# A four-layer convolution network on one core: layer 2's pass issued in the order of its text, with other lags and a split norm chain

## The chip, the core and the metric

The kernel runs on one core of one Trainium2 chip. The metric is the device time of one execution, in microseconds (us). Five engines of the core matter here: TensorE (PE) for matrix products and transposes, VectorE (DVE), ScalarE (ACT), GpSimd (POOL), and SyncE (SP), which issues every DMA of this kernel. Each engine has its own queue of instructions, and an instruction that needs another engine's result waits on a semaphore.

## The reference, cut to what matters

`x` has 16 images of 64 x 64 tokens with 256 channels. Four layers follow one another, each of the form `x = x + layer(group_norm(x))`:

```python
x = x + L0(_gn(x))   # linear attention with a layer norm
x = x + L1(_gn(x))   # gates per channel and per token, batch norm over all images, relu
x = x + L2(_gn(x))   # involution, 3 x 3, kernels made per token
x = x + L3(_gn(x))   # involution, 7 x 7, kernels made per token

def _gn(v, G=32, eps=1e-5):
    g = v.reshape(B_, H_, W_, G, C_ // G)
    m = jnp.mean(g, axis=(1, 2, 4), keepdims=True)
    s = jnp.var(g, axis=(1, 2, 4), keepdims=True)
    return ((g - m) / jnp.sqrt(s + eps)).reshape(v.shape)

# L2, K = 3, 16 groups of kernels
r = relu(bn(x @ Wr + br)); w = (r @ Ws + bs).reshape(B, H, W, 16, 1, 9)
# patches: nine shifted copies of (x @ Wi + bi), reshaped to (B, H, W, 16, 16, 9)
out = jnp.sum(w * patches, axis=-1)
```

Layer 1's batch norm needs sums over all images before its output can be made, and each group norm needs the sums of a whole image. So the kernel goes over the images in several passes.

## The kernel before, in words

The kernel has four stages. The first does layer 0 and gathers layer 1's maps, the second does layer 1's scan and its batch statistics, the third is layer 2's pass, and the last is layer 3. The change lies in the third stage, whose loop begins at line 1144.

The third stage cuts an image into 8 pieces of 512 tokens, so there are 128 pieces. One turn `n` of the loop works on four pieces at once, each of another age. `LAG = (0, 9, 17, 27)` says how old: `jobs(n)` (line 1127) gives the piece whose layer 1 is ended in this turn (`end`), the piece that is projected by `Wi` (`proj`, 9 turns later), the piece whose involution is computed (`inv`, 17 turns later), and the piece that is centred and stored in strips for layer 3 (`cen`, 27 turns later). The parts of a turn are these:

- `end_of_layer1` (line 891) is a generator with three parts. Part one is two DVE instructions (L899) that make `z`. Part two is two ACT relus (L905) and two POOL additions (L908) that make `x2`. Part three is two statistics of `x2` on DVE (L914), which wait for POOL. In the text before, part three of a turn stands near the start of the next turn.
- `projected` (L948 on PE, L952 on ACT) fills the lines of `pad`.
- `prepare` makes the next piece ready: `reduced2` (L969 on PE, L972 on ACT), 36 transposes of `pad` on PE in nine tiles `pt` (L995), copied by ACT to `xs` (L999, with short copies at L1001 and L1005), and `weights` (L979). It stands early in the turn, except where the next piece is the first of an image; there it stands after the products.
- `residual` (L1021, L1023) puts the piece's `x2` into the two accumulators `lo`. `products` multiplies patches and weights on DVE (24 instructions L1033 in a turn, 12 for each half). `sums` adds nine taps on DVE (L1045) and adds the result to `lo` (L1046). For a quarter of the first half, PE adds the taps (`sums_on_tensor`, L1050), and ACT copies that quarter to `x3` at the next turn (L1175).
- `turned` transposes the `x3` of the turn before (L1060 on PE, L1061 on ACT), and `statistics3` takes its statistics on DVE (L1080).
- `centred` subtracts the channel means `gmb` on POOL (L1103) and leaves 32 small DMAs to be issued by SP.

Twice in an image a norm chain runs: `norm2`, when the last piece of an image has ended layer 1, and `norm3`, when the last piece has its `x3`. Both begin with `group_norm` (line 109): DVE gathers statistics (L114), PE averages over groups (L117), DVE takes deviations (L119 to L123), PE averages again (L126), and DVE and POOL take the inverse root (L98, L99). `norm2` then scales the weights on DVE (L924, L925) and has a PE product `pm` (L931) and two DVE instructions (L936, L938). `norm3` ends with a PE product `pb` (L1095) and a DVE copy of it to `gmb` (L1098), a tile with a single buffer. The chains are generators too; each call of `step()` in the loop runs one more link of every chain that is open. A turn has six such calls, called S1 to S6 below, in the order of the text.

What sets the order on an engine: the framework's scheduler. It takes the text as a priority and orders each engine's instructions by its own model of time, so the order in the queues is not that of the text. It also hands out buffers.

The PSUM pools of this stage are `tr` with 2 buffers, `sm` with 1 (for the norm chains' small products and for `reduced2`), `pw` with 3 and `acc` with 2.

Of the kernel before, what the change touches and what calls it, by code (L numbers as in the profile page):

```python
# [9 lines left out]
F32 = mybir.dt.float32  # L10
# [3 lines left out]
PSUM = bass.MemoryType.PSUM  # L14

P = 128
C = 256
# [3 lines left out]
CT = 512  # L21
# [23 lines left out]
def network(ctx: ExitStack, tc: tile.TileContext, a: dict, out: bass.AP):  # L45
    nc = tc.nc
# [61 lines left out]

    def group_norm(stats, pool):


        mv = small.tile([P, 2, 2], F32, tag="gn_mv", name="gn_mv")
        for h in range(2):
            nc.vector.bn_aggr(mv[:, h, :], stats[:, h].rearrange("p n s -> p (n s)"))  # L114
        yield
        pg = pool.tile([P, CT], F32, tag="sm", name="pg")
        nc.tensor.matmul(pg[:, 0:2], lhsT=gmat, rhs=mv[:, :, 0], start=True, stop=True)  # L117
        gm = small.tile([P, 2], F32, tag="gn_m", name="gn_m")
        nc.vector.tensor_copy(gm, pg[:, 0:2])  # L119
# [29 lines left out]
    with ExitStack() as st:  # L149
# [304 lines left out]
        def gate1(i):  # L454

            mv, gm, rstd = yield from group_norm(st1.pop(i), sm)
            av = small.tile([P, 2, 2], F32, tag="av", name="av")
# [364 lines left out]
    with ExitStack() as st:  # L822
# [95 lines left out]
        def norm2(i):  # L918

            _, gm, rstd = yield from group_norm(st0.pop(i), sm)  # L920
            wrs = wk.tile([P, 2, 64], F32, tag="wrs", name="wrs")
# [4 lines left out]
            yield  # L926
            pm = sm.tile([P, CT], F32, tag="sm", name="pm")
            for f in range(3):
                for h in range(2):
                    lhsT = wrs[:, h] if f == 2 else w[:, h, f * P : (f + 1) * P]  # L930
                    nc.tensor.matmul(  # L931
                        pm[0 : 64 if f == 2 else P, f : f + 1], lhsT=lhsT, rhs=gm[:, h : h + 1],
                        start=(h == 0), stop=(h == 1),
                    )
            b2 = small.tile([64, 1], F32, tag="b2", name="b2")
            nc.vector.tensor_scalar(b2, pm[0:64, 2:3], sb2[0:64, 2:3], sb2[0:64, 1:2], ALU.mult, ALU.add)  # L936
# [25 lines left out]
        def reduced2(i, rc):  # L962
# [160 lines left out]

        LAG = (0, 9, 17, 27)
        TURNS = NI * NCH + LAG[3]

# [14 lines left out]

        loads(0)
        ahead, made, ending, last_end = None, None, None, None
        for n in range(TURNS):
            end, proj, inv, cen = jobs(n)
            nxt = jobs(n + 1)[2]
            done, stores[:] = list(stores), []
            loads(n + 1)
            for dst, src in done:
                nc.sync.dma_start(out=dst, in_=src)  # L1150
            nxt_cen = jobs(n + 1)[3]
            if nxt_cen:
                load_centred(*nxt_cen)
            now, ahead = ahead, None
            last_end, ending = ending, end_of_layer1(*end) if end else None
            if ending:
                next(ending)
            if last_end:
                next(last_end, None)
            if inv:  # L1160
                w1 = weights(now[1], 1)
                x3 = wk.tile([P, 4, C], F32, tag="x3", name="x3", bufs=3)
            step()

            def prepare():
                x2r, rt = reduced2(*nxt)
                ahead = [x2r, rt]
                ahead.append(patches(*nxt, lambda: ahead.append(weights(rt, 0))))
                return ahead

            if nxt and nxt[1]:
                ahead = prepare()
            step()
            if made:
                nc.scalar.copy(made[2][:, 0:ON_PE, 0:P], made[3][:, 0:ON_PE])  # L1175
            if ending:
                next(ending)
            if inv:
                los = residual(now[0])
            c3 = turned(*made[:3]) if made else None  # L1180
            step()
            if proj:
                projected(*proj)
            if inv:
                pd = products(0, now[2], now[3])
                sums_on_tensor(pd, los[0])
            step()
            if nxt and not nxt[1]:
                ahead = prepare()
            if inv:  # L1190
                pd1 = products(1, w1, now[3])
                sums(0, pd, los[0], x3)
            if made:
                statistics3(*made[:2], c3)
            step()
            if inv:
                sums(1, pd1, los[1], x3)
            made = (*inv, x3, los[0]) if inv else None
            step()
            if cen:  # L1200
                centred(*cen)
        for dst, src in stores:
            nc.sync.dma_start(out=dst, in_=src)

# [308 lines left out]
```

## Time and profile before

| quantity | us |
|---|---|
| median of 3 runs | 11259.85 |
| lowest and highest run | 11252.87, 11263.24 |
| the profiled execution's own time | 11230.29 |
| its span, first to last instruction | 11228.4 |
| first instruction L899 of layer 2's pass | 4169.2 |
| last instruction L1103 of layer 2's pass | 8019.5 |

Layer 2's pass takes some 3850 us of the 11228. The profiled execution is 29.6 us below the median of the runs; both of its numbers differ from each other by 1.9 us that lie around the span.

The views used below are these. The page's second part cuts the span into 40 slices of 281 us; layer 2's pass lies in slices 15 to 28, counted from zero. The table by windows gives the busy time of each engine in a stretch. The timeline lists instructions in order of time: start, duration, engine, line, operation, what is written and read, and in brackets the idle time before it with what ended it. The list of waits sums such idle times.

### The profile page before, as it was taken

The numbers are of one execution on the slowest core, as the hardware profiler recorded it, in microseconds if no ns is written. First come the engines' busy times: TensorE is split into PE (matmuls) and PEld (weight loads), VectorE is DVE, ScalarE is ACT, GpSimd is POOL, SyncE is SP. The second block draws the span as 40 slices with busy tenths as digits, with TensorE's granted clock in tenths as the row PEclk, the third lists the DMA queues.
The fourth block names the chain that finished last, engine by engine and source line by source line (L and its number), as shares of the span: only waits on it lengthen the run. The fifth ranks groups of instructions, "written<-read, shape, count | busy, mean of one in ns | idle before, by whom it ended". The sixth has DMA issues, their size and how long they took to land.

```text
span 11228.4 us, 218020 instructions
## 1 busy us (share of the span) xinstructions
PE 8510.5 (76%) x88184; PEld 6175.2 (55%) x88184; DVE 7531.5 (67%) x11694; ACT 4699.1 (42%) x10571; POOL 1065.1 (9%) x681
## 2 busy tenths in 40 slices
PE   8889888988886407777777777777277777778777
PEld 5666666666664205555555555555165656666555
DVE  5566656656665498988888888899254545555444
ACT  4555555555554004333333333333144444444444
POOL 0110111111110001111111111111000000000000
PEclk9999999999997558888888888888689998998988
DMA  7334334434432385555555555544356555555555
GB/s 239 129 134 148 130 122 146 139 128 133 145 101 84 106 279 177 160 169 165 163 159 167 160 168 164 163 151 141 107 177 202 185 194 179 179 181 176 195 185 171
DMA packets 1353714, 1796.58 MB, mean 160 GB/s; under 512 B 132875, under 2 KB 1031812, under 8 KB 1351556
## 3 DMA queue, kind: packets, MB, share of 16 engines
q1 hardware_dynamic: 1352708, 1782.63, 49.6%
q8 instruction: 697, 11.42, 0.4%
q14 instruction: 309, 2.53, 0.1%
HBM read 1268.05 MB, written 536.87 MB: 161 GB/s over the span
## 4 chain that ended last, share of the span: by engine, by line
PE 32%; DVE 20%; issue 17%; DMA 10%; ACT 9%; SPq 7%; POOL 4%; POOLq 0%; DVEq 0%; ACTq 0%
PE pa L1347 6%; DVE wm L1303 6%; SPq L1150 5%; PE pq L261 5%; PE pk L1288 4%; PE py L417 4%; DMA c_d<-c 3%; DVE x L1045 3%; PE pr L1256 2%; ACT sq L426 2%; ACT wm L1298 2%; DVE pd L1033 2%; PE px L948 2%; PE pt L995 2%; DMA xc<-x_d 1%
## 5 line engine op out<-in xcount | busy, mean ns | idle before, releaser
L261 PE MATMUL pq<-wq,xn 128*128 128x384 f32 x4096 | 1475.9, 500 | 59.8 <-DVE diag L310 20.9
L1033 DVE TENSOR_TENSOR pd<-xs,pw 128x576 f32<-128x576 f32 (+15 forms) x3072 | 1450.5, 544 | 47.7 <-ACT xs L1001 47.7
L1303 DVE TENSOR_TENSOR wm<-pk,spanb 128x704 f32<-128x704 f32 x896 | 1148.4, 1344 | 217.4 <-PE pk L1288 217.1
L1288 PE MATMUL pk<-rt,span 64*128 64x176 f32 x12288 | 1175.6, 329 | 153.5 <-DVE wm L1303 61.0
L1347 PE MATMUL pa<-wm,xw 126*32 126x48 f32 x45056 | 819.6, 227 | 474.2 <-issue 374.1
L1288 PEld LDWEIGHTS pk<-rt,span 64*128 64x128 f32 x12288 | 938.1, 188 | 385.7 <-ACT wm L1298 181.8
L1298 ACT ACTIVATE wm<-pk,spanb 128x176 f32<-128x176 f32 x2560 | 975.0, 542 | 337.8 <-PE pk L1288 328.9
L1045 DVE TENSOR_REDUCE x<-pd 128x384 f32<-128x3456 f32 (+1 forms) x256 | 1109.2, 4334 | 0.0
L1347 PEld LDWEIGHTS pa<-wm,xw 126*32 126x32 f32 x45056 | 679.8, 124 | 714.2 <-issue 516.7
L1357 DVE SCALAR_TENSOR_TENSOR ex<-pa,msk,ex 128x192 f32<-128x192 f32 x704 | 287.2, 416 | 1161.8 <-ACT ex L1356 1159.3
L261 PEld LDWEIGHTS pq<-wq,xn 128*128 128x128 f32 x4096 | 752.8, 194 | 492.5 <-issue 54.1
L995 PE MATMUL pt<-ident,pad 128*128 128x128 f32 x4608 | 759.7, 310 | 244.2 <-ACT pad L952 188.5
L995 PEld LDWEIGHTS pt<-ident,pad 128*128 128x128 f32 x4608 | 593.4, 160 | 422.0 <-ACT pad L952 234.2
L1050 PE MATMUL lo<-pd,ident 128*128 128x128 f32 x2304 | 568.0, 415 | 285.4 <-DVE pd L1033 285.4
L999 ACT COPY xs<-pt 128x512 f32<-128x512 f32 x1152 | 644.8, 586 | 299.1 <-PE pt L995 264.4
L1356 ACT ACTIVATE ex<-pa,msk 128x192 f32<-128x192 f32 x704 | 289.3, 420 | 1019.2 <-PE pa L1347 1016.1
L1050 PEld LDWEIGHTS lo<-pd,ident 128*128 128x128 f32 x2304 | 501.2, 268 | 335.6 <-DVE pd L1033 315.3
L948 PE MATMUL px<-x2p,wis 128*128 128x512 f32 x1024 | 571.7, 708 | 37.5 <-ACT c L1061 23.2
L972 ACT ACTIVATE rt<-pr,b,sb 64x512 f32<-64x512 f32 x128 | 98.9, 772 | 1077.3 <-PE pr L969 1017.5
L417 PE MATMUL py<-wo,oT 128*128 128x256 f32 x2048 | 482.4, 386 | 59.9 <-DVE va L277 45.2
L417 PEld LDWEIGHTS py<-wo,oT 128*128 128x128 f32 x2048 | 378.8, 191 | 135.3 <-PE po L380 49.0
L426 ACT ACTIVATE sq<-y 128x256 f32<-128x256 f32 x512 | 213.2, 416 | 520.2 <-DVE y L422 511.7
(229 smaller groups left out, 13427.4 us busy)
## 6 DMA issues: line engine op xcount, KB each, us to landing
xw<-strips SPq DMA_DIRECT2D x704, 512.0 KB
xn<-x_d SPq DMA_DIRECT2D x256, 512.0 KB
x<-x_d SPq DMA_DIRECT2D x256, 512.0 KB
x_d<-x SPq DMA_DIRECT2D x256, 512.0 KB
strips<-xc SPq DMA_DIRECT2D x3072, 28.0 KB
xin<-in_x SPq DMA_DIRECT2D x256, 256.0 KB
x_d<-xc SPq DMA_DIRECT2D x128, 512.0 KB
xm<-x_d SPq DMA_DIRECT2D x128, 512.0 KB
```

Of the source, the lines that this page charges most:

```text
L261: nc.tensor.matmul(pq[:, dd, 0:384], lhsT=xn[:, h, tok], rhs=wq[:, h, hf * 384 : (hf + 1) * 384], start=(h == 0), stop=(h == 1),)
L417: nc.tensor.matmul(py[:, q, :], lhsT=oT[hf][:, q * P : (q + 1) * P], rhs=wo[:, hf, :], start=(hf == 0), stop=(hf == 1),)
L948: nc.tensor.matmul(px, lhsT=w[:, h, fh * P : (fh + 1) * P], rhs=x2[:, h], start=(h == 0), stop=(h == 1),)
L995: nc.tensor.transpose(pt[:, k, h * P : (h + 1) * P], lines[:, h, rc * 4 + e + k, 2 * j : 2 * j + P], ident,)
L999: nc.scalar.copy(t[:, e : e + 2, 0:C], pt)
L1033: nc.vector.tensor_tensor(pd[:, :, o - oh * P : o - oh * P + n, :], xs[dj][:, di : di + 4, c0 : c0 + 9 * n].rearrange("p r (f k) -> p r f ...
L1045: nc.vector.tensor_reduce(half, pd[:, n:], AX.X, ALU.add)
L1050: nc.tensor.matmul(lo[:, 0:ON_PE], lhsT=ident, rhs=pd[:, 0:ON_PE, :, k], start=False, stop=(k == 8))
L1288: nc.tensor.matmul(pkv[:, b, m], lhsT=span[half, h * 8 + q * 2 + gg, s0 : s0 + P], rhs=rto[half, o, :], start=True, stop=True,)
L1298: nc.scalar.activation(dst[:, m // 2, m % 2], pkv[:, m // 2, m % 2], AF.Identity, bias=spanb[:, g0 + m : g0 + m + 1],)
L1303: nc.vector.tensor_tensor(dst, pkv, spanb[:, g0 : g0 + 4].rearrange("p (b m) -> p b m", b=2).unsqueeze(3).broadcast_to([P, 2, 2, NTL]), AL ...
L1347: nc.tensor.matmul(pav[32 * q : 32 * q + 32, :, tj * TC : (tj + 1) * TC], lhsT=xws[k][0:TILE_IN, tj, 32 * q : 32 * q + 32], rhs=wm[q][0:TI ...
```

## The change

Three things change in layer 2's pass.

1. The whole loop stands in `tc.manual_schedule()`. Inside it every engine, SP with its DMAs included, issues its instructions in the order of the text. Buffers are still handed out by the scheduler.
2. The norm chains of this pass are split: `apart=True` puts a link on PE and the DVE link that reads its result at different calls of `step()`, and one call without work follows the inverse root. The lags become `(0, 10, 18, 29)`, so there are 157 turns where there were 155. The pool `sm` goes, and its tiles come from `tr`, which has 3 buffers now.
3. Part three of `end_of_layer1` moves from the start of the next turn to the end of its own turn, after `sums(1, ...)`. Part two now stands ahead of the ACT copy L1175, which stood ahead of it.

The diff, without the lines of the loop that are only indented and without the calls in layers 0 and 1, which pass `"sm"` as the tag:

```diff
-    def group_norm(stats, pool):
+    def group_norm(stats, pool, tag, apart=False):
         mv = small.tile([P, 2, 2], F32, tag="gn_mv", name="gn_mv")
         for h in range(2):
             nc.vector.bn_aggr(mv[:, h, :], stats[:, h].rearrange("p n s -> p (n s)"))
         yield
-        pg = pool.tile([P, CT], F32, tag="sm", name="pg")
+        pg = pool.tile([P, CT], F32, tag=tag, name="pg")
         nc.tensor.matmul(pg[:, 0:2], lhsT=gmat, rhs=mv[:, :, 0], start=True, stop=True)
+        if apart:
+            yield
         gm = small.tile([P, 2], F32, tag="gn_m", name="gn_m")
...
         yield
-        pv = pool.tile([P, CT], F32, tag="sm", name="pv")
+        pv = pool.tile([P, CT], F32, tag=tag, name="pv")
         nc.tensor.matmul(pv[:, 0:2], lhsT=gmat, rhs=dev, start=True, stop=True)
+        if apart:
+            yield
         rstd = small.tile([P, 2], F32, tag="gn_r", name="gn_r")
         inv_sqrt(rstd, pv[:, 0:2], GN_EPS)
         yield
+        if apart:
+            yield
         return mv, gm, rstd
...
-        tr = st.enter_context(tc.tile_pool(name="b_tr", bufs=2, space=PSUM))
-        sm = st.enter_context(tc.tile_pool(name="b_sm", bufs=1, space=PSUM))
+        tr = st.enter_context(tc.tile_pool(name="b_tr", bufs=3, space=PSUM))
...
-            _, gm, rstd = yield from group_norm(st0.pop(i), sm)
+            _, gm, rstd = yield from group_norm(st0.pop(i), tr, "tr", apart=True)
...
-            pm = sm.tile([P, CT], F32, tag="sm", name="pm")
+            pm = tr.tile([P, CT], F32, tag="tr", name="pm")
...
+            yield
             b2 = small.tile([64, 1], F32, tag="b2", name="b2")
...
-            pr = sm.tile([P, CT], F32, tag="sm", name="pr")
+            pr = tr.tile([P, CT], F32, tag="tr", name="pr")
...
-            _, gm, rstd = yield from group_norm(st3.pop(i), sm)
+            _, gm, rstd = yield from group_norm(st3.pop(i), tr, "tr", apart=True)
...
-            pb = sm.tile([P, CT], F32, tag="sm", name="pb")
+            pb = tr.tile([P, CT], F32, tag="tr", name="pb")
...
+            yield
             nc.vector.tensor_copy(gmb[i], pb[:, 0:C])
...
-        LAG = (0, 9, 17, 27)
+        LAG = (0, 10, 18, 29)
...
+        with tc.manual_schedule():
...
-                last_end, ending = ending, end_of_layer1(*end) if end else None
+                ending = end_of_layer1(*end) if end else None
                 if ending:
                     next(ending)
-                if last_end:
-                    next(last_end, None)
...
-                if made:
-                    nc.scalar.copy(made[2][:, 0:ON_PE, 0:P], made[3][:, 0:ON_PE])
                 if ending:
                     next(ending)
+                if made:
+                    nc.scalar.copy(made[2][:, 0:ON_PE, 0:P], made[3][:, 0:ON_PE])
                 if inv:
                     los = residual(now[0])
...
                 if inv:
                     sums(1, pd1, los[1], x3)
+                if ending:
+                    next(ending, None)
                 made = (*inv, x3, los[0]) if inv else None
                 step()
```

A turn of the text after the change runs so: the loads of the next turn, the stores of the turn before and the load for the next `centred`; part one of `end_of_layer1`; `weights` for the second half; S1; `prepare`, if the next piece isn't the first of an image; S2; part two of `end_of_layer1`; the copy L1175; `residual`; `turned`; S3; `projected`; `products` of half 0; `sums_on_tensor`; S4; `prepare`, if the next piece is the first of an image; `products` of half 1; `sums` of half 0; `statistics3`; S5; `sums` of half 1; part three of `end_of_layer1`; S6; `centred`.

More of the change, by code (lines that the diff above doesn't have):

```diff
@@ L232, in norm0 @@
         def norm0(i):
-            _, gm, rstd = yield from group_norm(st0.pop(i), sm)
+            _, gm, rstd = yield from group_norm(st0.pop(i), sm, "sm")
             nb = small.tile([P, 2], F32, tag="gn_b", name="gn_b")
@@ L454, in gate1 @@
         def gate1(i):
-            mv, gm, rstd = yield from group_norm(st1.pop(i), sm)
+            mv, gm, rstd = yield from group_norm(st1.pop(i), sm, "sm")
             av = small.tile([P, 2, 2], F32, tag="av", name="av")
@@ L918, in norm2 @@
         def norm2(i):
-            _, gm, rstd = yield from group_norm(st0.pop(i), sm)
+            _, gm, rstd = yield from group_norm(st0.pop(i), tr, "tr", apart=True)
             wrs = wk.tile([P, 2, 64], F32, tag="wrs", name="wrs")
@@ L1140, in loads @@
                 load_layer1(*end)
[L1142 to L1149, printed above, removed]
-                nc.sync.dma_start(out=dst, in_=src)
[L1151 to L1154, printed above, removed]
-            last_end, ending = ending, end_of_layer1(*end) if end else None
-            if ending:
-                next(ending)
-            if last_end:
-                next(last_end, None)
[L1160 to L1173, printed above, removed]
-            if made:
-                nc.scalar.copy(made[2][:, 0:ON_PE, 0:P], made[3][:, 0:ON_PE])
[L1176 to L1201, printed above, removed]
@@ L1202, in network, with prepare @@
-        for dst, src in stores:
-            nc.sync.dma_start(out=dst, in_=src)
+        with tc.manual_schedule():
+            loads(0)
+            ahead, made = None, None
+            for n in range(TURNS):
+                end, proj, inv, cen = jobs(n)
+                nxt = jobs(n + 1)[2]
+                done, stores[:] = list(stores), []
+                loads(n + 1)
+                for dst, src in done:
+                    nc.sync.dma_start(out=dst, in_=src)
+                nxt_cen = jobs(n + 1)[3]
+                if nxt_cen:
+                    load_centred(*nxt_cen)
+                now, ahead = ahead, None
+                ending = end_of_layer1(*end) if end else None
+                if ending:
+                    next(ending)
+                if inv:
+                    w1 = weights(now[1], 1)
+                    x3 = wk.tile([P, 4, C], F32, tag="x3", name="x3", bufs=3)
+                step()
+                def prepare():
+                    x2r, rt = reduced2(*nxt)
+                    ahead = [x2r, rt]
+                    ahead.append(patches(*nxt, lambda: ahead.append(weights(rt, 0))))
+                    return ahead
+                if nxt and nxt[1]:
+                    ahead = prepare()
+                step()
+                if ending:
+                    next(ending)
+                if made:
+                    nc.scalar.copy(made[2][:, 0:ON_PE, 0:P], made[3][:, 0:ON_PE])
+                if inv:
+                    los = residual(now[0])
+                c3 = turned(*made[:3]) if made else None
+                step()
+                if proj:
+                    projected(*proj)
+                if inv:
+                    pd = products(0, now[2], now[3])
+                    sums_on_tensor(pd, los[0])
+                step()
+                if nxt and not nxt[1]:
+                    ahead = prepare()
+                if inv:
+                    pd1 = products(1, w1, now[3])
+                    sums(0, pd, los[0], x3)
+                if made:
+                    statistics3(*made[:2], c3)
+                step()
+                if inv:
+                    sums(1, pd1, los[1], x3)
+                if ending:
+                    next(ending, None)
+                made = (*inv, x3, los[0]) if inv else None
+                step()
+                if cen:
+                    centred(*cen)
+            for dst, src in stores:
+                nc.sync.dma_start(out=dst, in_=src)
```

## The prediction

> **What bounds the kernel now.** I read the page's slices first, then a table by windows, then the timeline of single turns. The change touches layer 2's pass alone (slices 15 to 28); there DVE is the busiest engine:
>
> ```profile
> DVE  5566656656665498988888888899254545555444
> ```
>
> Windows of that pass: an early turn, a later turn, twice eight turns (one image), and a turn at the end, when layer 1 has run out. The columns are the window, its length, then busy time (and count) of PE, PEld, DVE, ACT, POOL, clock, DMA share, GB/s.
>
> ```profile
> 4335.04:4359.64 24.60, 21.06 (x98) 15.48 (x99) 23.92 (x35) 10.09 (x20) 2.51 (x2) 0.86 0.43 146
> 5301.53:5328.98 27.45, 20.33 (x99) 14.88 (x99) 24.70 (x35) 10.20 (x21) 4.81 (x3) 0.88 0.57 174
> 5424.11:5658.94 234.83, 171.76 (x814) 123.03 (x814) 204.65 (x298) 81.29 (x163) 39.89 (x26) 0.84 0.53 161
> 5658.94:5895.20 236.26, 170.30 (x814) 120.65 (x814) 204.60 (x299) 82.19 (x163) 39.93 (x26) 0.85 0.55 166
> 7623.69:7645.60 21.91, 18.80 (x101) 13.07 (x100) 21.91 (x31) 8.51 (x18) 2.36 (x1) 1.00 0.54 161
> ```
>
> So an image takes 235.5 us, of which DVE works 204.6 and idles some 30. Where it idles, DVE's timeline of the later turn tells:
>
> ```profile
> 5306.38 0.75 DVE L1033 TENSOR_TENSOR pd<-xs,pw 128x576 f32<-128x576 f32 x1
> 5307.05 0.68 DVE L1046 TENSOR_TENSOR x<-x,lo 128x512 f32<-128x512 f32 x1
> 5307.64 10.56 DVE L1033 TENSOR_TENSOR pd<-xs,pw 128x468 f32<-128x468 f32 x23
> 5318.13 0.74 DVE L899 SCALAR_TENSOR_TENSOR z<-x,gm,pf 128x512 f32<-128x512 f32 x1
> 5318.90 0.75 DVE L899 SCALAR_TENSOR_TENSOR pf<-x,gm,pf 128x512 f32<-128x512 f32 x1
> 5321.84 0.69 DVE L914 BATCH_NORM_STATS2 st<-x 128x6 f32<-128x512 f32 x1 [2.18 <-POOL x L908]
> 5323.06 0.69 DVE L914 BATCH_NORM_STATS2 st<-x 128x6 f32<-128x512 f32 x1 [0.53 <-POOL x L908]
> 5323.68 3.74 DVE L1045 TENSOR_REDUCE x<-pd 128x384 f32<-128x3456 f32 x1
> ```
>
> The scheduler puts the statistics L914 right behind their own `z`, and DVE waits 2.7 us for ACT and POOL. The list of waits for an image names the same:
>
> ```profile
> DVE st L914 <- POOL x L908: 22.1, 15, 4.1
> DVE b L936 <- PE pm L931: 3.2, 1, 3.2
> DVE pd L1033 <- ACT xs L1001: 2.7, 2, 1.7
> ```
>
> PE's blocks in that pass, for the queue walk below (matmul records are twice the matmuls in f32):
>
> ```profile
> 5312.69 4.39 PE L1050 MATMUL lo<-pd,ident 128*128 128x128 f32 x18 [2.15 <-DVE pd L1033]
> 5317.01 1.93 PE L969 MATMUL pr<-x2r,wrs 128*64 128x512 f32 x4
> 5319.81 2.00 PE L979 MATMUL pw<-ws,rt 65*128 65x72 f32 x16 [0.87 <-ACT rt L972]
> 5321.68 3.70 PE L948 MATMUL px<-x2p,wis 128*128 128x512 f32 x8
> ```
>
> [...] So in text order one waiting matmul holds all of PE's later work; the [2.15 <-DVE pd L1033] above shows PE so held. [...] with waits before it the block L948 took up to 6.63 us (at 5382.63) against 3.70. [...] here the POOL additions take 1.26 to 1.28 us beside DVE's products too (4347.39), so I count nothing for it.
>
> **The change part by part.** *Steady turn, statistics moved.* The early turn is 24.5 us of DVE without the wait. Text order costs a little: L1046 follows its own reduce directly. Starts 5389.90 and 5394.88 lie 4.98 apart where the second depends on the first, 4.86 (5358.28, 5363.14) where another stands between; 0.12 for each of two pairs. So a turn is 24.7 us if nobody keeps DVE waiting, against 27.45. The additions for L914 are then done some 15 us before DVE comes to them.
>
> *Does the text keep PE in time?* From DVE's start T of a turn: z to 1.3, half 0 of L1033 to 6.9, half 1 to 12.5, reduce to 16.3. There L1046 needs PE's L1050 (an early turn shows it waiting for PE, 0.27 us at 4333.96). PE in text order: ACT's relus end at 2.2, L1175 at 2.5, `residual` 1.4 (eight transposes like L1060's 1.2) to 4.0, `turned` 1.2 to 5.2, L948 to 8.9, L1050 to 13.3; three us to spare. Then `weights` 1.0, L969 1.9, nine tiles paced by ACT (nine copies of 0.55, three short ones of 0.23, the relu of rt 0.77, PE's second `weights` 1.0 between): 9.1 from L969 to ACT's end. PE's and ACT's whole loop is 23.2, only 1.5 below DVE's 24.7. SP: a turn without layer 1 is 21.0 us of issuing (7604.7 to 7625.7), five DMAs of 0.5 more and the wait for the last strips make about 25, below the mean turn found next.
>
> *The chains* are where text order bites. With m = n mod 8:
> - m=0: PE's pg stands at S1, ahead of `prepare`; its statistics come at the very end of DVE's turn m=7. PE stands idle some 10 us, starts `prepare` at T+0.5 instead of T-10, and everything behind it is late: ACT's relus 11.0 (behind the copies), `residual`, `turned`, pv at 14.4. DVE wants pv at S4, behind half 0, at 7.7: stall 6.8. [...] Links' own work: 1.9 (four at 0.2, one 0.2, L924/L925 0.9). Turn 34.9.
> - m=1: pm waits for L925 at the turn's end; DVE 0.7 more. 25.4.
> - m=2: the late `prepare` of m=1 and the early one of m=2 follow each other on PE; L1050 ends at 19.1, wanted at 16.3: stall 2.9, L114 0.6. 28.2.
> - m=3: pg holds PE until L114; pv comes behind `prepare`, at 3.8, wanted at 2.1: stall 1.8[...], links 1.7. 28.7.
> - m=4: the copy L1098 to `gmb` stands at S1, but `gmb` has one buffer, and POOL reads the old one in `centred` of piece 7 of the image before, which falls into this same turn (28+8i with lag 29), at its end. Before, the copy came a good 20 us after that read (5449.83+2.35, then 5472.42), free of charge. Now DVE waits behind ACT's copies (4.1), relus, two additions of 1.27 and `centred` 2.35: to 9.9, from 1.3: 8.6[...]. 34.7.
> - m=5, 6: 24.7 each. m=7: 25.4.
>
> Sum 226.7 against 235.5: 8.8 less an image. Eleven images lie so (turns from 4718 to 7308): -97. In the first sixteen turns before had hardly a wait (199.1 and 208.6 us for eight, L1045 to L1045); with the same stalls but no `centred` I get +22. The last 23 turns, where L914 is gone: about +5. Two turns more: one at the start, 7 us (z to z is 5 to 7), one of strips alone at the end, 15.2 (five from 7907.8 to 7983.9). Sum: -97 + 22 + 5 + 22 = -48.
>
> Against the profiled execution's own 11230.3 that is 11182; it lies 29.6 below the median of the runs, and since the pass has the same shape I move the median alike: 11260 - 48 = **11212**.
>
> **Costs not seen before.** The wait for `gmb`: 5.2 if PE isn't late, 8.6 as walked, nothing if the wait isn't there; I take 8.6, since one buffer excludes nothing. The stall on pv: 0 if PE reaches S3 by 7.7, 10 if `prepare` is slow; 6.8. A third `tr` buffer: gains at most 0.1 a tile (pairs of tiles come 1.33 apart, the copies alone 1.07), or loses 3 us an image if a pt gets the slot that pg holds; I take 9.1 for `prepare`. The links moved apart cost SP nothing; SP's loads stand behind the wait for `x2p`'s buffer (projected at T+9 to 19), one turn before they are needed.
>
> **The rivals.**
> - Gapless: the split chains hide every wait. For: that is 204.6 busy of 234.8 already. Against: pg ahead of `prepare`. An image is 8 x 24.7 + 5.5 = 203, 32 less; eleven give -354, the rest about -12: 10894.
> - `gmb` doesn't wait, the rest as forecast: -11 x 9.6: 11212 - 106 = 11106.
> - Slower: the PE and ACT loop paces every turn. In an early turn ACT took 9.7 us from the relu of rt to the last short copy (4334.81 to 4344.55), where I count 7.2; such a loop is 25.7. Then PE never catches up after a link, and L1046 waits in every turn. With 26 the image is 8 x 26 + 25 (pg 8, pm 9, pg and pb 5, gmb 3) = 233: -27 over eleven, +40 early, +12 late, +22: +47, 11307. It decides from a loop of about 25.5.
> - The whole is no change: the -48 needs only 4 us more an image.
>
> **How the numbers follow.** Forecast 0.50 (its own range 11120 to 11270), `gmb` free 0.10, gapless 0.15, slower 0.25. The range takes in the forecast, the free `gmb` and the slow loop, 11060 to 11330, and leaves out gapless. A measurement of this kernel tells no change from about 0.2%, 22 us: faster 0.63 (most of the forecast, gapless, `gmb` free), same 0.12, slower 0.25.
>
> **What would show it.** L914 without a wait for POOL, and turns of 24.7 between chains: the moved statistics. L98 waiting for pv some 7 us once an image, L1046 waiting for L1050 at m=2, and L1098 waiting for POOL L1103 some 8 us: the text's price. If the sum of DVE's idle time is under 8 us an image, gapless is right; if L1046 waits for PE in every turn, the slow loop is. The forecast is wrong if PE reaches pv early, or SP's queue starves z.

## The result, and the profile after

The kernel after the change takes 11302.34 us (median of 7 runs, 11286.83 to 11311.8) where the kernel before takes 11259.85. The ratio is 1.0037, with a 95% interval of 1.0025 to 1.0049: the change makes the kernel slower by 0.37%, 42.5 us. The forecast was 48 us faster.

The profiled execution of after took 11310.92 us (span 11309.1), 80.7 more by its span than the one of before. Of these, 35 lie in layer 2's pass and 46 in layer 3, whose code is the same: there single profiled executions differ (3139 to 3185 us from its first `wm` to the end, over all kernels of this study). The medians differ by 42.5, so the 35 of the pass would be most of it. The pass, cut at the starts of the 128 long reduces (128x512, L1045 before, L1051 after):

| stretch of the pass | before, us | after, us | difference | forecast |
|---|---|---|---|---|
| span's start to first long reduce | 4310.4 | 4311.6 | +1.2 | +7 |
| first two images | 407.8 | 429.0 | +21.3 | +22 |
| eleven full images | 2590.2 | 2549.4 | -40.8 | -97 |
| the rest, to the last long reduce | 567.9 | 578.6 | +10.7 | +5 |
| last long reduce to layer 3's first `wm` | 212.9 | 255.3 | +42.5 | +15.2 |
| sum | | | +35.0 | -48 |

So the first two images came out as forecast, the start and the end of the images each missed by some 6 us, the full images won less than half of what they should, and the tail (the last row but one) lost almost three times its price. That the tail's 42.5 equals the difference of the medians is chance.

What the move of the statistics was meant to remove is gone. DVE's timeline in a turn without a chain, after (columns as before: start, duration, engine, line, operation, what is written and read):

```profile
5509.02 1.28 DVE L919 BATCH_NORM_STATS2 st<-x 128x6 f32<-128x512 f32 x2
5510.22 0.73 DVE L904 SCALAR_TENSOR_TENSOR z<-x,gm,pf 128x512 f32<-128x512 f32 x1
5510.99 0.75 DVE L904 SCALAR_TENSOR_TENSOR pf<-x,gm,pf 128x512 f32<-128x512 f32 x1
5511.65 8.44 DVE L1039 TENSOR_TENSOR pd<-xs,pw 128x576 f32<-128x576 f32 x18
```

No bracket stands at L919, and none at the other instructions of that turn: DVE works without a pause, and the turn is 24.9 us (forecast 24.7) instead of 27.45. Run e7 below asks whether it was the move that did this. The table by windows for one image, and the list of DVE's waits in the same stretch:

```profile
5433.20:5665.30 232.10, 171.15 (x814) 128.54 (x814) 202.10 (x299) 81.71 (x162) 40.02 (x26) 0.82 0.54 166
```

```profile
DVE isq L98 <- PE pv L128: 16.5, 2, 9.0
DVE gmb L1105 <- POOL xc L1110: 11.3, 1, 11.3
DVE b L942 <- PE pm L936: 0.7, 1, 0.7
```

DVE idles 232.1 - 202.1 = 30 us of an image, as much as before. The 22.1 us of waiting for POOL's additions are gone, and 28.5 us of waiting in the two chains have come. The timeline shows the first wait of `norm3`. PE first:

```profile
5433.39 0.56 PE L117 MATMUL pg<-gn_mv,gmat 128*128 128x2 f32 x2 [4.43 <-DVE gn_mv L114]
...
5435.70 3.27 PE L975 MATMUL pr<-x2r,wrs 128*64 128x512 f32 x4
...
5441.54 1.73 PE L1001 MATMUL pt<-ident,pad 128*128 128x128 f32 x8 [1.99 <-DVE gn_m L121]
...
5449.25 0.28 PE L128 MATMUL pv<-gn_d,gmat 128*128 128x2 f32 x2
```

DVE in the same stretch, with the wait for the means' buffer a turn later:

```profile
5441.34 0.15 DVE L121 COPY gn_m<-pg 128x2 f32<-128x2 f32 x1
...
5449.57 0.16 DVE L98 TENSOR_SCALAR isq<-pv 128x2 f32<-128x2 f32 x1 [7.50 <-PE pv L128]
...
5486.45 0.42 DVE L1105 COPY gmb<-pb 128x256 f32<-128x256 f32 x1 [11.25 <-POOL xc L1110]
```

PE stands 4.43 us before `pg`, whose input DVE makes late in its turn. All of `prepare` follows `pg` in the text, and it now starts late and runs slowly (`pr` 3.27 us, where 1.93 was read before). A transpose `pt` then waits 1.99 us more for the buffer that `pg` holds until DVE reads it at L121. Only behind all this comes `pv`, and DVE has waited 7.50 us for it.

In the tail SP's queue stands still (engine SPq, the issue of DMAs; x32 is a count):

```profile
7801.63 15.35 SPq L1158 DMA_DIRECT2D strips<-xc  x32
7841.38 0.40 SPq L1225 DMA_DIRECT2D wr<-in_w_reduce  x1
7841.82 0.47 SPq L1225 DMA_DIRECT2D span<-in_span  x1
7842.52 1.51 SPq L872 DMA_DIRECT2D xc<-x_d  x2
```

L1225 loads constants of layer 3, code that stands below the loop. The scheduler, which still orders what lies outside the loop, put such loads among the loop's own transfers, here the first two of them. The first waits 24 us, from 7816.98 to 7841.38 (SP's list of waits names PE's product `pw`, L985, of the loop), and the loads and stores of the last turns wait behind it.

### The profile page after: what moved, and what is told of

Read it like the earlier page. It is cut to its first block, busy times and chain, and to the rows that moved or that the text cites. A ratio compares the mean times of both kernels' runs of the same rounds, so it can differ in the third digit from the quotient of the medians.

```text
span 11309.1 us, 218547 instructions
## 1 busy us (share of the span) xinstructions
PE 8498.6 (75%) x88184; PEld 6264.6 (55%) x88184; DVE 7501.0 (66%) x11694; ACT 4692.4 (41%) x10571; POOL 1064.8 (9%) x681
## 4 chain that ended last, share of the span: by engine, by line
PE 35%; DVE 21%; issue 13%; DMA 11%; ACT 9%; SPq 7%; POOL 3%; DVEq 0%; ACTq 0%; POOLq 0%
PE pa L1355 6%; DVE wm L1311 6%; SPq L1158 6%; PE pq L267 5%; PE pk L1296 4%; PE py L423 4%; DVE pd L1039 3%; DMA c_d<-c 3%; PE px L954 2%; DVE x L1051 2%; DMA x_d<-x 2%; PE pr L1264 2%; ACT sq L432 2%; ACT wm L1306 2%; SPq L872 2%
## 5 line engine op out<-in xcount | busy, mean ns | idle before, releaser
L1051 DVE TENSOR_REDUCE x<-pd 128x384 f32<-128x3456 f32 (+1 forms) x256 | 1110.0, 4336 | 0.0
L1005 ACT COPY xs<-pt 128x512 f32<-128x512 f32 x1152 | 608.9, 587 | 149.1 <-PE pt L1001 146.7
L1001 PE MATMUL pt<-ident,pad 128*128 128x128 f32 x4608 | 633.2, 293 | 34.1 <-DVE gn_m L121 22.7
L1001 PEld LDWEIGHTS pt<-ident,pad 128*128 128x128 f32 x4608 | 541.9, 151 | 209.0 <-issue 131.0
L1056 PE MATMUL lo<-pd,ident 128*128 128x128 f32 x2304 | 554.2, 410 | 56.5 <-DVE pd L1039 56.5
L1056 PEld LDWEIGHTS lo<-pd,ident 128*128 128x128 f32 x2304 | 480.9, 218 | 160.3 <-DVE pd L1039 69.2
L954 PE MATMUL px<-x2p,wis 128*128 128x512 f32 x1024 | 529.5, 664 | 8.8 <-ACT pf L910 5.0
L1029 PE MATMUL lo<-ident,x2r 128*128 128x128 f32 x896 | 204.4, 361 | 398.5 <-ACT x L1183 247.9
L117 PE MATMUL pg<-gn_mv,gmat 128*128 128x2 f32 x128 | 29.5, 300 | 620.9 <-DVE gn_mv L114 615.9
```

The source lines that it names most:

```text
L954: nc.tensor.matmul(px, lhsT=w[:, h, fh * P : (fh + 1) * P], rhs=x2[:, h], start=(h == 0), stop=(h == 1),)
L1001: nc.tensor.transpose(pt[:, k, h * P : (h + 1) * P], lines[:, h, rc * 4 + e + k, 2 * j : 2 * j + P], ident,)
L1051: nc.vector.tensor_reduce(half, pd[:, n:], AX.X, ALU.add)
L1056: nc.tensor.matmul(lo[:, 0:ON_PE], lhsT=ident, rhs=pd[:, 0:ON_PE, :, k], start=False, stop=(k == 8))
```

## The experiments

All ratios are to runs of the kernel before on the same chip; "image" is the time of eight long reduces in the middle of the pass, in the profiled execution.

| run | what it is | median, us | ratio [95%] | image, us |
|---|---|---|---|---|
| before | | 11259.85 | 1 | 235.5 |
| after | the change | 11302.34 | 1.0037 [1.0025, 1.0049] | 232.1 |
| e5_statlate | before, statistics moved, scheduler's order | 11261.43 | 0.9998 [0.9989, 1.0007] | 235.5 |
| e7_textonly | before, text order | 11238.45 | 0.9980 [0.9973, 0.9988] | 227.0 |
| e4_nomanual | after, scheduler's order | 11342.58 | 1.0088 [1.0073, 1.0103] | 242.3 |
| e1_sp | after, SP's order kept | 11271.34 | 1.0024 [1.0014, 1.0034] | as after |
| e2_gmb2 | after, two `gmb` buffers | 11188.29 | 0.9944 [0.9926, 0.9962] | 225.3 |
| e3_links | after, first product later | 11141.57 | 0.9908 [0.9895, 0.9922] | 217.6 |
| e6_all | e1, e2 and e3 together | 11128.51 | 0.9881 [0.9867, 0.9896] | 213, then 220 |
| e9_lags | e6 with lags 0, 9, 17, 27 | 11105.17 | 0.9863 [0.9847, 0.9880] | 212, then 220 |
| e10_pool | e9, a quarter of the strips by POOL | 10970.70 | 0.9749 [0.9735, 0.9764] | 211.5 |
| e10b_act | e9, a quarter of the strips by ACT | 11485.93 | 1.0211 [1.0196, 1.0227] | 249 |
| e11_textgmb2 | e7 with e1 and e2, chains not split | 11169.65 | 0.9932 [0.9915, 0.9948] | 223 |

### Which part does what

**The statistics alone (e5).** The call stands at the end of its turn, the scheduler still orders.

```diff
-            if last_end:
-                next(last_end, None)
...
                 sums(1, pd1, los[1], x3)
+            if ending:
+                next(ending, None)
```

> The kernel before, with the third part of the end of layer 1 (the statistics of x2) moved to the end of its own turn in the text, and nothing else; the scheduler still orders every engine. Theory: the place in the text does nothing, since the scheduler puts the statistics right behind their own z again: DVE waits for POOL some 22 us an image as before, the image stays at 235 to 236 us, the time within 0.2% of the kernel before. Rival: the move does the work and the text order is not needed: the waits for POOL vanish and the image falls by 15 us or more, the time by 1.5% or more.

Nothing changed, 0.9998. The first line of DVE's waits in an image of it:

```profile
DVE st L914 <- POOL x L908: 24.0, 15, 4.1
```

The scheduler goes by its own times and puts the statistics back behind their `z`. Moving a step in the text says nothing until the text is what orders the queue.

**The text order alone (e7).** The loop of the kernel before, only indented under `tc.manual_schedule()`.

> The kernel before, with its loop issued in the order of its text, and nothing else: chains not split, lags 9, 17, 27, the pool of one buffer kept, the statistics at the start of the next turn. Theory: the text order is what removes the waits for POOL (turns of 24.9 without a chain), and chains that are not split stall DVE about as long as the split ones of the change, some 20 us an image (pg 2, pv 5, pm 5, pb 1, the wait for the means' buffer 6), so that an image is near 224 to 232 us; with one strips-only turn and one lead-in turn less than in the change, the time is 11200 to 11300. Rival: the split is needed under the text order, each answer of PE is awaited behind PE's whole queue (5 to 10 us for each of six answers): an image of 245 us or more, a time of 11420 or more.

The theory held: 0.9980, image 226 to 228 us, turns of 24.9 between the chains. DVE's waits in one image:

```profile
DVE gmb L1098 <- POOL xc L1103: 15.9, 1, 15.9
DVE isq L98 <- PE pv L126: 2.7, 1, 2.7
DVE b L936 <- PE pm L931: 2.2, 1, 2.2
DVE rs L1088 <- POOL gn_r L99: 0.7, 1, 0.7
DVE gn_m L119 <- PE pg L117: 0.7, 1, 0.7
```

No wait for POOL's additions is left, with the statistics still at the start of the next turn. So the order of the text is what removes it; that the change also moves the statistics won nothing that a run shows (e5 has the move without the order). The chains' waits are 22.2 us, less than the 28.5 of the change. Apart from the means' buffer the chains that are not split wait 6.3 us, the split ones 17.2. Text order is the part of the change that gains; the rest of it (the split with its lags and its pool, the moved statistics, the later copy L1175) costs 0.6%.

**The rest without the text order (e4).** `with tc.manual_schedule():` becomes `if True:`, all else as in the change.

> The changed kernel without the manual schedule: split links, new lags, three buffers and the moved statistics stay, but the scheduler orders the engines. Theory (the text's order of the chain links on PE and DVE makes the waits for pv and gmb): these waits are gone or small, waits of DVE for POOL at the statistics of x2 are back if the scheduler draws them forward again; close to the kernel before plus two turns, 11260 to 11290 us. Rival (the split links and lags cost by themselves): as slow as the changed kernel or slower, 11300 and up.

1.0088: slower than after and than before, as the rival had it. DVE's largest entry in an image of it:

```profile
DVE st L919 <- POOL x L913: 36.0, 10, 5.9
```

The chains' own waits are small here; the loss stands at the statistics, 36.0 us where e5 has 24.0. So with either order the split, its lags and its pool together cost: 0.9% under the scheduler, 0.6% in text order (1.0037 against 0.9980). Text order is worth 0.2% with the old chains and 0.5% with the split ones.

### What the waits of the change are worth

**Two buffers for the means (e2).** `bufs=1` becomes `bufs=2` at `gmb`.

> Only the buffers of gmb change, 2 for 1, so that the copy to gmb need not wait for the read of the image before. Theory (each DVE wait of the chains costs what it shows): the wait of 11.3 us an image goes; PE is late in that turn, so some 3 us come back as the addition after the reduce waiting for PE's tap sums: 8 us an image, 11 images, about 11215 us. Rival (the loop of PE and ACT paces the chain turns, the gmb wait only covers PE's lateness): the full 11 us come back as that wait for PE, no change, 11300.

0.9944, some 105 us below after, where the theory had 85. DVE's waits in an image:

```profile
DVE isq L98 <- PE pv L128: 16.2, 2, 8.6
DVE x L1052 <- PE lo L1056: 5.0, 1, 5.0
DVE b L942 <- PE pm L936: 0.7, 1, 0.7
```

The 11.3 us at `gmb` are gone, but the image wins only 6.8, because a wait for L1056 of 5.0 us appears in the same turn, 20 us after the copy to `gmb` (at 5451.48):

```profile
5471.71 0.55 DVE L1052 TENSOR_TENSOR x<-x,lo 128x384 f32<-128x384 f32 x1 [5.02 <-PE lo L1056]
```

PE is late in that turn (m=4), and in after the longer wait for the buffer had covered it.

**The first product of each chain later (e3).** One call of `step()` more ahead of `pg` in `norm2`, two in `norm3`.

```diff
-    def group_norm(stats, pool, tag, apart=False):
+    def group_norm(stats, pool, tag, apart=False, late=0):
...
         yield
+        for _ in range(late):
+            yield
         pg = pool.tile([P, CT], F32, tag=tag, name="pg")
```

> Only the places of the chain links change: one empty call after the statistics in norm2 and two in norm3, so that PE's first group product comes behind prepare and no longer ahead of it. Theory (PE standing idle ahead of prepare is what makes everything behind it late): both waits for pv (7.5 and 9.0 us an image) go, the wait for gmb falls from 11.3 to about 5; an image takes some 210 us for 232, in all about 11020 us. Rival (PE and ACT are at their pace anyway, so the lateness comes back as the addition after the reduce waiting for PE's tap sums, or SP's queue starves the turn): less than 100 us, 11200 or more.

0.9908, between the two expectations. DVE's waits in an image:

```profile
DVE gmb L1107 <- POOL xc L1112: 3.5, 1, 3.5
DVE b L944 <- PE pm L938: 2.0, 1, 2.0
```

Both waits for `pv`, 16.5 us, are gone with one edit that lets `prepare` stand ahead of `pg` on PE. That the chain's place on PE was their cause is shown; as every later link moves along with `pg`, and PE's standing, the slower run of `prepare` and the buffer held by `pg` go together, the shares of these are not shown. The image won 14.5; the buffer of the means still waits, 3.5 us here, and 8.9 and 16.6 in two of the last images.

**SP's order kept (e1).** A second region, for SP alone, from the loop to the constants of layer 3, so that the scheduler can't move these loads up.

```diff
+        sp_text = ExitStack()
+        sp_text.enter_context(tc.manual_schedule(engines={mybir.EngineType.SP}))
         with tc.manual_schedule():
             loads(0)
...
         sb3 = folded(pc, "l3", "L3_mean", "L3_var", "L3_gamma", "L3_beta", None)
+        sp_text.close()
```

> Only SP's order changes: layer 3's constant loads come after the last strips in SP's queue, where the changed kernel has the first of them among the strips of the last pieces, waiting 24 us for PE. Theory (SP paces the tail, so a wait there is paid in full): the 24 us wait goes, the strips end some 25 us earlier, the constants cost some 10 us again ahead of layer 3; 11285 us or a little below (11302 before). Rival (the loss is in layer 3, which took 46 us longer in the profile though its code is the same): nothing in the tail matters, 11300, and layer 3 still takes about 3185 us.

1.0024 against 1.0037: the intervals overlap, so the medians alone show little. In the profile the tail is 239.8 us instead of 255.3, and the pause is gone; SP then issues these loads behind the last strips:

```profile
8041.17 13.43 SPq L1213 DMA_DIRECT2D strips<-xc  x32
8054.71 0.40 SPq L1227 DMA_DIRECT2D wr<-in_w_reduce  x1
```

The 24 us pause was worth 15.6, for early constants had also saved something: in e1 all of these loads stand between the last strips and layer 3's first loads and take SP 8.2 us (8054.71 to 8062.88).

### Together, and what is behind it

**All three (e6).**

> The change with three amendments together: two buffers for the means, the first product of both chains one or two calls later, and SP's order kept through the constants of layer 3. Theory: their gains add, but for the part in which they cover one another. With the later links alone the image was 217.6, of which 3.5 was the wait for the means' buffer (10 and more in the last images): the image falls to 214, the last reduce comes some 80 us earlier than with the later links alone, and the tail is 240 as with SP's order alone; in all 11030 to 11050. Rival: the wait for the means' buffer covered waits of PE, as it did when the second buffer stood alone (11.3 removed, 6.8 gained): the image stays at 216 or above, the time is 11070 to 11110.

11128.51, 0.9881: both expectations missed. The first full images are 213 to 214 us, as the theory had it, but from the seventh image on they are 218 to 224, with turns of 26 to 33 where 24.9 was the rule. PE's timeline there:

```profile
6089.99 3.65 PE L977 MATMUL pr<-x2r,wrs 128*64 128x512 f32 x4 [5.01 <-DMA x2r<-x_d]
6117.93 3.65 PE L977 MATMUL pr<-x2r,wrs 128*64 128x512 f32 x4 [5.68 <-DMA x2r<-x_d]
```

PE waits for a load of the piece's own `x2`, and SP issues one transfer after another, with no pause over 1.8 us in the whole image:

```profile
6108.84 1.27 SPq L874 DMA_DIRECT2D xc<-x_d  x2
...
6110.80 0.43 SPq L874 DMA_DIRECT2D x2r<-x_d  x1
...
6114.72 2.47 SPq L1162 DMA_DIRECT2D x_d<-x  x3
6117.86 1.04 SPq L1162 DMA_DIRECT2D c_d<-c  x2
6119.19 13.66 SPq L1162 DMA_DIRECT2D strips<-xc  x24
```

The image from 6036 on takes 219.2 us, 27.4 a turn, and this was read as SP's own length of a turn; e10 tests it. That the first images run faster was read as a lead of SP that is used up. The lists of issues fit: in the image from 5170 (212.7 us) SP issued 349 transfers, 0.61 us each, and in the one from 6036 360, again 0.61 us each. An image has 360, so in the faster images SP fell behind by some eleven transfers an image.

**The old lags (e9).** `LAG` goes back to `(0, 9, 17, 27)`.

> The same three amendments with the lags of the kernel before, 9, 17 and 27 turns, so 155 turns in place of 157. Theory: what the two turns cost is their own length: 7 us at the start and a turn of strips alone of 16.4 at the end, and the turns between stay as they are: 20 to 25 us below the kernel with the three amendments and lags 10, 18, 29; from the last reduce to layer 3 it is 16 us less. Rival: the lags of the change are needed for its chains: with 17 the late preparation of an image's first piece falls into the turn of the chain of norm 2, whose products then wait behind it, 5 us or more an image, and the time is 50 us or more above that kernel.

11105.17, 23 us below e6, as the theory said. With their first products later, the split chains do not need the lags of the change. The tail is 17.6 us shorter (252.8 to 235.2): that is one turn of strips.

**A quarter of the strips issued by POOL (e10).** This is the test of SP as the bound. By its place in the list a store of `x2` or `x3` goes along with the eight strips of a turn.

```diff
-                for dst, src in done:
-                    nc.sync.dma_start(out=dst, in_=src)
+                for k, (dst, src) in enumerate(done):
+                    (nc.gpsimd if k % 4 == 1 else nc.sync).dma_start(out=dst, in_=src)
```

> The kernel with the three amendments and the old lags, with every fourth of the 32 strip DMAs of a turn issued by POOL in place of SP. Theory: from the sixth image on SP's queue bounds that kernel: it issues without a gap, 27.4 us a turn, and PE's product for the reduced map waits for the load of x2r. With eight strips less (0.45 us each, 3.6 us) SP needs 23.8, below DVE: all full images come back to 211 to 213 us, the last reduce some 75 us earlier, the time 11020 to 11045. Rival: the bytes bound the turns, or what POOL now does ahead of its additions keeps DVE waiting: images of 218 or more as before, time within 0.3% of the kernel with the old lags or above it.

10970.70 us, 0.9749 [0.9735, 0.9764], further than expected. Every full image takes 210.8 to 212.3 us. The window of one of them:

```profile
6004.80:6215.80 211.00, 164.34 (x832) 124.27 (x831) 206.14 (x299) 82.69 (x165) 79.46 (x98) 0.85 0.58 182
```

DVE idles 5 us of an image. POOL's busy time, its issuing counted, doubles to 79 of 211 us, which it has to spare. No PE instruction waits for `x2r` in it, though more bytes move per second than in after or in e6's image from 6036 (182 against 166 and 175 GB/s). SP now has time to wait for other engines:

```profile
SPq L1162 <- POOL xc L1112: 16.4, 2, 9.2
SPq L874 <- PE px L956: 15.4, 6, 4.6
```

So SP's queue was the bound, not the bytes. The last long reduce comes 95 us earlier than in e9. The tail falls too, from 235.2 to 190.3 us: POOL issues a share of the strips, and turns of strips alone lie some 13 us apart where e9 has 16.4. That SP also carries no backlog into the tail is likely, but not shown apart. This version beats both kernels, by 2.5% and 2.9%.

**The same by ACT (e10b).** `nc.scalar` in place of `nc.gpsimd`.

> The same, but the eight strips are issued by ACT. Theory (SP is the bound, and ACT, busy 80 us of an image, has room): images of 211 to 213, as with POOL. Rival: these eight stand ahead of ACT's copies at the start of a turn, and the loop of PE and ACT has little slack: 3.6 us later in every turn, so that DVE waits for PE and turns are 27 or more, images 218 or more.

1.0211: the rival was right about the direction, at twice its size, with images of 246 to 253 us. Eight strips cost ACT 4.76 us of issue, and it waits before them too, for POOL to make the tile that they store. In one turn:

```profile
6302.51 2.35 POOL L1112 TENSOR_TENSOR xc<-xc,gmb 128x1024 f32<-128x1024 f32 x1 [12.68 <-DMA xc<-x_d]
6304.88 5.01 ACTq L1162 DMA_DIRECT2D strips<-xc  x8
```

ACT's last instruction before this issue ended at 6293.8, so its queue stood for 11 us, and the relu of `rt` behind it came at 6309.95. ACT's waits in an image:

```profile
ACT rt L980 <- DMA x_d<-x: 51.3, 3, 17.3
ACT rt L980 <- PE pr L977: 37.7, 3, 16.5
ACT rt L980 <- DMA strips<-xc: 22.8, 2, 16.1
```

The names in this list are of what came last by the profile, and mix: the wait shown above stands there as one for `pr`. PE waits for `x2r` here as well, 84.5 us in a stretch of 432. What holds that load stays open.

**Chains not split, the rest amended (e11).** e7 with the edits of e1 and e2.

> The kernel before with its loop in text order, two buffers for the means and SP's order kept through layer 3's constants; its chains are not split, the lags are 9, 17, 27, the statistics stand at the start of the next turn. Theory: the split of the chains is not needed: of the image of 227 us that text order alone gave, 16.2 were the wait for the means' buffer; the early images fall to 211 to 213, the later ones to SP's 27.4 us a turn, 218 to 220, and the time is within 0.3% of the kernel with the split, the old lags and the amendments (0.986 of before). Rival: the wait covered waits for PE, as in the change, where 11.3 went and 6.8 were gained; then a later split is worth something: early images of 217 or more, the time 40 us or more above.

The rival was right: 0.9932, an image of 222 to 224, where e9 has 0.9863 and early images of 212. With the buffer free the same instruction waits for PE instead:

```profile
5435.61 0.60 PE L1095 MATMUL pb<-dg,ones 128*128 128x256 f32 x2
```

```profile
5423.85 0.48 DVE L1092 TENSOR_SCALAR dg<-ident,gm 128x128 f32<-128x128 f32 x2
5436.24 0.43 DVE L1098 COPY gmb<-pb 128x256 f32<-128x256 f32 x1 [11.91 <-PE pb L1095]
```

DVE has made `dg` at 5424.3 and wants `pb` at once, while PE has a whole `prepare` ahead of it, from 5423.02 on. Of the 15.9 us that e7 waited for the buffer, 11.9 lay over this wait. With the buffer free an image is 223 us with the chain not split, 225.3 with the split and its first product ahead of `prepare` (e2), and 212 to 214 with that product behind it (e6, e9). So the split seems to pay where its first product stands behind `prepare`. It is not shown alone: the split chains also have another pool. In e11 `pr` waits 2.25 us until DVE has read `pv` from the single buffer of `sm`, which holds up the `prepare` that `pb` stands behind.

## Why the prediction was wrong

Two terms of the sum failed. The waits of DVE in the chains were sized too small, so that an image gained 3.7 us where 8.8 was counted (97 us in eleven images, measured 40.8), and the tail was given the price of one turn of strips, 15.2 us, where 42.5 was measured.

- **The bound, right; its remedy, credited to the wrong part.** The forecast named the 22 us of POOL waits as what there was to win; they are gone, the turn is 24.9 us. It put this down to "the moved statistics", but the order of the text alone does it (e7), and the move alone does nothing (e5). In its first two images after loses 21.3 us, 22 in the forecast; this agreement was not taken apart.
- **The image, wrong in size; this is the larger failure.** The term is "Sum 226.7 against 235.5: 8.8 less an image". Measured is 232.1 in most images, and eleven images won 40.8 us instead of 97: 56 us missing. The mechanism, PE held at a link by the text, was right, and it stood in the working; its waits were sized wrong. Three of the walk's turns also carry the author's own estimate for a slower PE: 1.5 us at m=0, 0.5 at m=3, 1.0 at m=4. At m=3 "stall 1.8", 2.3 with this estimate, was 7.5, for `pv` came 9.4 us into the turn (5449.25, the turn's `z` at 5439.90) where the walk had 3.8: the walk let `prepare` end early in turn m=3, where it starts behind a held `pg` and runs slowly, and it did not take up the loss "if a pt gets the slot that pg holds", which the trace shows as 1.99 us of wait. For `gmb`, 8.6 + 1.0, 11.3 was measured. At m=0 6.8 + 1.5 was forecast, and 9.0 came. At m=2 "stall 2.9" did not come: in after L1056 ends at 5661.06, 14.4 us into that turn, where the walk had 19.1. PE's lateness at L1056 showed two turns later, at m=4, once `gmb` was free (5.0 us in e2). The waits sum to 28.5 where 23.8 were counted (8.3 + 0.7 + 2.9 + 2.3 + 9.6); with the longer turn, 0.2 us eight times, that is 6.3, a little more than the 5.4 by which the image is longer.
- **The tail, wrong.** The term is "one of strips alone at the end, 15.2". Measured is 42.5. Three parts make it. The extra turn of strips is 16.4 us by the spacing of the last turns after (17.6 between e6 and e9). SP's pause costs 15.6 (e1). The ten other turns of strips take 16.4 us instead of 15.2 each, which makes about 12. Together they are 44, near the 42.5. The longer turn shows in SP's queue, first before, then after:

```profile
7924.26 13.80 SPq L1150 DMA_DIRECT2D strips<-xc  x32
7938.23 1.24 SPq L867 DMA_DIRECT2D xc<-x_d  x2
```

```profile
7927.80 13.77 SPq L1158 DMA_DIRECT2D strips<-xc  x32
7942.79 1.24 SPq L872 DMA_DIRECT2D xc<-x_d  x2
```

SP pauses 0.2 us ahead of the load of the next `xc` before, and 1.2 after, where the load stands directly behind the strips whose landing it waits for. Text order alone, with no turn more, has a tail of 239.9 us (e7), 27 above before; with SP's order kept as well (e11) it is 220.0. So there the pause is worth 20 and the ten turns 7. The forecast asked what SP's loads wait for inside the loop, and not what the scheduler would put from below the loop into SP's queue.
- **SP's load, too low.** "about 25, below the mean turn found next": it needs 27.4, as e6 and e9 show and e10 confirms. In after, with 29.0 us a turn, that hides; it limits each repair of the change.
- **The rivals.** The slow loop of PE and ACT, the way in which "slower" was foreseen, did not come: turns between chains are 24.9. That its 11307 us and its image of 233 lie near the measured 11302 and 232.1 is luck, for its mechanism is absent. The kernel is slower for sizes inside the likeliest case and for a pause that no case had. `gmb` free was counted at 9.6 us an image; e2 gained 71 us in the eleven images (2549.4 to 2478.0), 6.5 each.
- **GpSimd beside DVE, not the same beside every instruction.** The forecast counted nothing here, from additions beside DVE's products. Where an addition of before met an instruction L899, which makes `z`, it took 1.39 to 1.60 us in six cases of seven, against 1.26 to 1.28 in all others; why is not shown. No wait of the result turns on this.

The granted clock goes with the slow runs of `prepare`. In after PE is idle from 5428.97 to 5433.39, the granted clock is 0.50 from 5431.60 to 5438.43, and `pr`, which runs from 5435.70 on, takes 3.27 us where it took 1.93. Of the 128 runs of `pr` in after 46 took over 3.1 us, at a mean granted clock of 0.50 to 0.60; the 82 others took under 2.0, at 1.00. What lowers the clock is not shown. The forecast's 0.5 us at m=3, an estimate, was for one block, though a whole `prepare` follows.

## What to carry to other kernels

When a loop is put in the order of its text, the order alone can remove waits that moving a line under the scheduler does not (e7 and e5). Then walk each queue past every link that answers another engine: a product whose input comes late belongs behind the long independent block, not ahead of it, and its reader a step further on. An order written by hand ends where its region ends, and what lies outside can still be put into the same queue, so look for such instructions at both ends. After one wait is gone look for the next (here a single buffer, then the order of two products, then the queue that issues the DMAs), and ask of each buffer wait which other wait it covers.

## What the runs showed of the hardware

- A queue that issues small DMAs bounded a kernel whose bytes fit: SP took 13.66 us for 24 strips of 22 to 28 KB in e6, gaps included, and its turn of 27.4 us set the pace while the DMA engines were 55 to 58% busy. With nine transfers of each turn moved to POOL (eight strips in 4.31 us there) the same engines moved 182 GB/s instead of 175.
- The same eight strips on ACT took 4.76 us and made the kernel 4.7% slower than on POOL (1.0211 against 0.9749). There the issuing queue also waited for what its transfers wait for: ACT stood 11 us for POOL's tile, with the relu that `prepare` needs behind it. How much of the 4.7% this makes is not shown.
- An addition of GpSimd that met an instruction L899 of DVE took 1.39 to 1.60 us instead of 1.27 (before, six cases of seven).
